# An attention and graph-convolution kernel: the output's scaling in two parts, one split earlier, and another order for the last two batches

## The chip, the cores and the metric

The kernel runs on one core of one Trainium2 chip. The metric is device time in microseconds; 0.2% of it (5.6 us) is about what a measurement of this kernel can tell from no change. Five engines work side by side, each through its own queue in order: TensorE (PE, with weight loads as PEld) multiplies matrices into the eight banks of PSUM, VectorE (DVE), ScalarE (ACT) and GpSimd (POOL) work element by element, and SyncE (SP) issues the transfers (DMA). [...]

## The reference

32 batches `x` of 512 rows by 512 features in float32 and one adjacency matrix `adj` (512 x 512, zeros and ones) that all share. Two layers follow each other, each with a residual and a normalisation of rows:

```python
# layer 0: masked attention of 8 heads of 64
q, k, v = x @ Wq + bq, x @ Wk + bk, x @ Wv + bv
scores = q k^T / 8 + where(adj == 0, -1e9, 0)
x = layernorm(x + softmax(scores) v)
# layer 1: graph convolution
x = layernorm(x + (adj @ x) @ weight + bias)
```

## The kernel before, in words

**Tiling.** A batch is four blocks of 128 rows (`NB`), its features four blocks of 128 (`DB`). Each of the three projections and the convolution with the weight is one Strassen-Winograd product of 2 x 2 blocks of 256: seven products (`block_product`, L369) of eight matmuls of 128x256 each, put together by additions on VectorE and GpSimd. A product's bank is emptied by VectorE (L391 to L404 in `project`, L537 and L541 in `convolve`) or ScalarE (L394, L535). `combine_rows` (L331 to L333, GpSimd) makes three of the seven left factors from the blocks of `xT` or `yT`.

**Attention.** The 8 heads are four pairs (`hp`), and two pairs are a group (`g`), so a batch has two groups. `scores` makes k q for a pair and block of keys (L568), VectorE adds the mask (L570), ScalarE exponentiates (L572), and GpSimd adds the four key blocks (L583); the second pair's additions are kept in `later`. `attend` multiplies with v (L592). `fold_squares` (L623, L625) and `add_up` (L633, L636) turn those sums into reciprocal row sums, `inverse`. `turn_out` brings a pair's output back to rows: VectorE transposes squares of 32 (L606) and sixteen small DMAs (L611) put them in place, in the tile `rows`. The second groups of batches 30 and 31 go another way: ScalarE copies the output (L603), and TensorE transposes it (L655).

**Residual.** `residual(b, hp)` scales `rows` by `inverse`, eight ScalarE instructions of 128x64 for a pair (L650), and adds them to `X[b]` on GpSimd (L651). In the other way VectorE does both from PSUM (L656, L657).

**Convolution.** Normalised rows are split into a high part in the rounded format float32r and a low rest: `split_high` on ScalarE (L457), `split_low` on VectorE (L461), which also adds the bias on GpSimd (L462). `aggregate` multiplies both parts with the adjacency (L488), four times for a batch; ScalarE copies the result to `yT` (L491), VectorE makes one more factor (L493). `convolve` is the product with the weight. Its first product also goes into the tile `mix` (ScalarE, L535), besides VectorE's addition to `X[b]` (L541); products 6 and 7 are added to `mix` (L537). Its order is 1, 2, 5, 6, 7, 3, 4.

**Order of the work.** The program fixes each engine's order by hand (`manual_schedule`): an engine runs its instructions in the order in which the program lists them. The loop goes over the 64 groups. It lists the group's attention, then the scores of the next group, then `units` of other batches' work:

- first group of batch b: projections q, k and the first two of v for batch b + 1, with statistics and normalisations of batches b - 1 and b - 2 in between;
- second group: the rest of v for batch b + 1, the four splits and aggregations of batch b - 1, its convolution, and the transposes (`turn_squares`, L353) of batch b + 2.

`units_of(b)` makes the list, `weighed` gives the units weights in steps of about half, and `work_until` takes them off until a share of the group's weight is done: 0.85 in the first group, 0.6 in the second. Then the two pairs' residuals come, then the rest. The second group's residuals therefore stand behind the fourth aggregation and in front of the convolution; the first group's behind the thirteenth projection. The fourth split stands behind the last of v.

The last batch has no projections. It takes batch 29's convolution and batch 30's aggregations in its first group's list, all of them before the last attention; batch 30's statistics come with its last residual, its normalisation and three of its `split_high` at the end of its list, and two `split_low` in the first attention of batch 31. After the loop come the last residuals, batch 30's convolution, and batch 31's normalisation, aggregation by rows (`aggregate_rows`, L515) and convolution.

Of the kernel before, what the change touches and what calls it, by code (L numbers as in the profile page):

```python
# [41 lines left out]
AF = mybir.ActivationFunctionType  # L42
# [5 lines left out]
P = 128  # L48
HD = 64
# [11 lines left out]
GROUP = 4  # L61
# [146 lines left out]
def fast_kernel(ctx: ExitStack, tc, verdict, x, adj, Wq, bq, Wk, bk, Wv, bv, W1, b1, out):  # L208
    nc = tc.nc
    B, N, D = x.shape  # L210
    H = Wq.shape[1] // HD
    HP = H // 2
    NB = N // P
    DB = D // P
# [8 lines left out]
    def bank(*shape):  # L223

        return psum.tile([P, *shape], FP, name="bank", tag="bank", bufs=8)


    X, IN = {}, {}
# [177 lines left out]
    def flips(b):  # L406

        return [(turn_squares if b else x_transpose, b, c) for c in range(NB)] + [(sum_rows, b)] if b < B else []
# [16 lines left out]
    def statistics(b, which, c):  # L425
        if b + which not in STAT:
            STAT[b + which] = work.tile([P, 2 * NB, 2], FP, name="stat", bufs=3)
            RSTD[b + which] = work.tile([P, 2 * NB], FP, name="rstd", bufs=3)
            SHIFT[b + which] = work.tile([P, 2 * NB], FP, name="shift", bufs=3)
        st = work.tile([P, nc.vector.BN_STATS_DIM], FP, name="bnst")  # L430
        nc.vector.bn_stats(st, X[b][:, c, :])  # L431
        nc.vector.bn_aggr(STAT[b + which][:, which * NB + c, :], st)  # L432
# [118 lines left out]
    def convolution(b):  # L551
        return [(convolve, b, i) for i in (1, 2, 5, 6, 7, 3, 4)] if b >= 0 else []
# [3 lines left out]
    PAIRS = GROUP // 2  # L556
# [41 lines left out]
    def turn_out(b, hp):  # L598

        po = OUT.pop((b, hp))  # L600
        at = AT[b, hp] = work.tile([P, N], FP, name="attT")
        if b >= B - 2 and hp >= PAIRS:
            nc.scalar.activation(at, po, AF.Copy)  # L603
            return

        nc.vector.transpose(at, po)  # L606
        turned = at.rearrange("p (c j f) -> p c j f", c=NB, j=P // SQ)
        rows = ROWS[b, hp] = work.tile([P, NB, P], FP, name="rows")
        for i in range(P // SQ):
            for j in range(P // SQ):  # L610
                nc.sync.dma_start(rows[j * SQ:(j + 1) * SQ, :, i * SQ:(i + 1) * SQ],  # L611
                                  turned[i * SQ:(i + 1) * SQ, :, j, :])
# [24 lines left out]
        nc.vector.tensor_add(sums, pm, sums)  # L637
        nc.gpsimd.tensor_add(inverses, inverses, inverse)

    def residual(b, hp):  # L640
        at = AT.pop((b, hp))
        first = 2 * hp % GROUP
        inverse = INVERSE[b, 2 * hp // GROUP][:, :, first:first + 2]
        cols = X[b][:, :, hp * P:(hp + 1) * P]
        if (b, hp) in ROWS:
            rows = ROWS.pop((b, hp))
            for c in range(NB):
                for s in range(2):
                    part = rows[:, c, s * HD:(s + 1) * HD]
                    nc.scalar.activation(part, part, AF.Identity, bias=zero, scale=inverse[:, c, s:s + 1])  # L650
            nc.gpsimd.tensor_add(cols, cols, rows)  # L651
        else:
            pt = bank(NB, 2, HD)
            for c in range(NB):
                nc.tensor.transpose(pt[:, c, :, :], at[:, c * P:(c + 1) * P], ident)  # L655
            nc.vector.tensor_mul(pt, pt, inverse[:, :, :, None].to_broadcast([P, NB, 2, HD]))  # L656
            nc.vector.tensor_add(cols, pt.rearrange("p c s d -> p c (s d)"), cols)  # L657
        if hp == HP - 1 and b == B - 2:
            for c in range(NB):
                statistics(b, 0, c)  # L660


    def judge():
# [12 lines left out]
    def run(units):  # L676
        for unit in units:
            unit[0](*unit[1:])
# [15 lines left out]
    def norm(t, which):  # L694

        if t - which < 0:
            return []
        lo, hi = which * NB, (which + 1) * NB
        return [(square_root, t, slice(lo, hi)), (invert_root, t, slice(lo, hi))] + [
            (normalise, t, slot) for slot in range(lo, hi)]  # L700

    def folds(b, g):
        return [(fold_squares, b, hp) for hp in range(g * PAIRS, (g + 1) * PAIRS)]

    def survey(b):

        return [(statistics, b, 1, c) for c in range(NB)] if b >= 0 else []

    def weighed(units):

        weight = {project: 0.5, aggregate: 0.55, x_transpose: 0.13, convolve: 0.5}
        return [(u, weight.get(u[0], 0.0)) for u in units]

    def units_of(b):

        made, turned = projections(b + 1), flips(b + 2)
        splits, gathered = aggregation(b - 1)
        young, old, seen = norm(b - 1, 0) if b < B - 1 else [], norm(b - 1, 1), survey(b - 2)
        ready = [(turn_over, b)] if 1 < b < B - 1 else []
        if b == B - 1:  # L720


            older = convolution(b - 2)
            lows = [(split_low, b - 1, d) for d in range(DB - 1)]
            last = folds(b, 1)
            units = weighed(older[:3] + last[:1] + lows[2:] + splits[3:] + older[3:] + gathered + last[1:] + seen)
            return units, [sum(w for _, w in units)] * 2

        fresh = [(statistics, b - 1, 0, c) for c in range(NB)] if young else []
        if old:  # L730
            behind = [seen[:2], seen[2:], old[:2], old[2:4] + fresh[:2], old[4:] + ready + fresh[2:]] + [
                [u] for u in young]
        else:
            behind = [ready + fresh] + [[u] for u in young]
        if b == 0:
            behind = [[]] + [[(sum_weights, w1, n)] for n in range(4)]
        behind += [[] for _ in range(11 - len(behind))] + [splits[:1], [], splits[1:2]]
        behind += [[] for _ in range(16 - len(behind))]
        units = []
        for k, unit in enumerate(made[:16]):  # L740
            units += [unit] + behind[k]
        first = sum(w for _, w in weighed(units))
        values = made[16:]
        looked = [(look_for_low_half, c) for c in range(NB)] if b == 0 else []
        units += values[:3] + looked[:2] + gathered[:1] + splits[2:3] + gathered[1:2] + values[3:] + looked[2:] + splits[3:]
        if b == B - 2 > 0:
            units += [(load, B - 1)]
        units += gathered[2:3] + turned[:1] + gathered[3:]
        convolved = convolution(b - 1) if b < B - 2 else []
        for k in range(7):  # L750
            units += convolved[k:k + 1] + (turned[k + 1:k + 2] if k < 3 else turned[4:] if k == 6 else [])
        units = weighed(units)
        return units, [first, sum(w for _, w in units)]

    GROUPS = H // GROUP
    groups = [(b, g) for b in range(B) for g in range(GROUPS)]
    for i, (b, g) in enumerate(groups):
        if g == 0:
            units, ends = units_of(b)
            done = 0.0  # L760

        def release():
            run(later)
            later.clear()

        def work_until(part):

            nonlocal done
            begin = ends[g - 1] if g else 0.0
            while units and (units[0][1] == 0 or done < begin + (ends[g] - begin) * part - 0.3):  # L770
                unit, w = units.pop(0)
                if unit[0] == fold_squares and unit[2] % PAIRS:
                    release()
                run([unit])
                done += w
                if unit[0] == (project if b < B - 1 else convolve):
                    if b == B - 1 or unit[3] == 7:
                        release()

        for hp in range(g * PAIRS, (g + 1) * PAIRS):  # L780
            attend(b, hp)
            if i < len(groups) - 1:
                fold_squares(b, hp)
            turn_out(b, hp)
            if hp == 0:
                run(flips(1) if i == 0 else [(split_low, b - 1, d) for d in range(2)] if i == len(groups) - 2 else [])
        if i == len(groups) - 1:
            add_up(b, g)
            break
        later = scores(*groups[i + 1])  # L790
        add_up(b, g)
        if g == 0 and b + 2 < B:
            load_squares(b + 2)
        work_until(0.6 if g else 0.85)
        for hp in range(g * PAIRS, (g + 1) * PAIRS):
            residual(b, hp)
        work_until(1.0)
        if g == GROUPS - 1:
            run([u for u, _ in units])
            if b == B - 2:  # L800
                run(norm(b, 0) + [(split_high, b, d) for d in range(DB - 1)])
        release()
    t = B - 1
    rest, last = convolution(t - 1), convolution(t)
    for hp in range(HP - PAIRS, HP):
        residual(t, hp)
    run(rest[:1])
    old, seen = norm(t - 1, 1), survey(t - 1)
    run(old[:1] + rest[1:2] + old[1:])
# [75 lines left out]
```

## Time and profile before

Time before: 2789.32 us, median of three runs (2787.78 to 2789.43); the profiled run's span is 2785.0 us.

| engine | busy us | share of the span | instructions |
|---|---|---|---|
| TensorE, matmuls | 2752.0 | 99% | 12850 |
| TensorE, weight loads | 1917.2 | 69% | 12850 |
| VectorE | 2033.2 | 73% | 3349 |
| GpSimd | 1898.1 | 68% | 1221 |
| ScalarE | 1406.0 | 50% | 2447 |

The 16 DMA engines are busy 22.8% of the span with 139.10 MB, much of it in small packets. The granted TensorE clock is 0.996. "L541 DVE" is the VectorE instruction of line 541; "x31" says how many there are. In a line with "|", the first numbers after it are busy us and mean ns of one, and the next the engine's idle time in front of it, with what ended it behind "<-". In a timeline the first number is the start in us from the span's start, the second how long the merged group ran, and an idle time of the engine in front of it stands in brackets. A matmul's duration in the trace is its latency, longer than its distance from the next; so what a stretch of TensorE costs is read from start to start.

### The profile page before, as it was taken

The numbers are of one execution on the slowest core, as the hardware profiler recorded it, in microseconds if no ns is written. First come the engines' busy times: TensorE is split into PE (matmuls) and PEld (weight loads), VectorE is DVE, ScalarE is ACT, GpSimd is POOL, SyncE is SP. The second block draws the span as 40 slices with busy tenths as digits, with TensorE's granted clock in tenths as the row PEclk, the third lists the DMA queues.
The fourth block names the chain that finished last, engine by engine and source line by source line (L and its number), as shares of the span: only waits on it lengthen the run. The fifth ranks groups of instructions, "written<-read, shape, count | busy, mean of one in ns | idle before, by whom it ended". The sixth has DMA issues, their size and how long they took to land. (4 is left out here: it accounts for less than half of the span.)

```text
span 2785.0 us, 39215 instructions
## 1 busy us (share of the span) xinstructions
PE 2752.0 (99%) x12850; PEld 1917.2 (69%) x12850; DVE 2033.2 (73%) x3349; ACT 1406.0 (50%) x2447; POOL 1898.1 (68%) x1221
## 2 busy tenths in 40 slices
PE   9999999999999999999999999999999999999997
PEld 6666766767767667667676676676766766767755
DVE  6777676687776777767867667777677676687777
ACT  2455544654545555445545455454555544654554
POOL 4666776767766668676677676677666767667764
PEclk9999999999999999999999999999999999999999
DMA  5112212222122222122221222211222212222111
GB/s 146 29 31 58 46 27 56 59 60 55 23 50 57 61 56 41 32 56 61 58 57 18 54 59 60 56 27 46 57 61 57 43 30 56 60 59 56 31 37 48
DMA packets 588305, 141.66 MB, mean 51 GB/s; under 512 B 549952, under 2 KB 554048, under 8 KB 588096
## 3 DMA queue, kind: packets, MB, share of 16 engines
q1 hardware_dynamic: 588096, 139.10, 22.8%
q8 instruction: 103, 1.69, 0.3%
q14 instruction: 106, 0.87, 0.1%
HBM read 72.88 MB, written 33.55 MB: 38 GB/s over the span
## 5 line engine op out<-in xcount | busy, mean ns | idle before, releaser
L572 ACT ACTIVATE e<-e 128x1024 f32<-128x1024 f32 x512 | 524.0, 1052 | 542.1 <-DVE e L570 516.4
L583 POOL TENSOR_TENSOR es<-es,e 128x1024 f32<-128x1024 f32 x256 | 617.7, 2413 | 20.1
L570 DVE SCALAR_TENSOR_TENSOR e<-gap,bank 128x512 f32<-128x512 uint8 x1024 | 616.7, 677 | 12.2 <-PE bank L568 12.2
L583 POOL TENSOR_TENSOR es<-e 128x1024 f32<-128x1024 f32 x128 | 316.1, 2469 | 302.3 <-ACT e L572 302.3
L568 PE MATMUL bank<-q,k 64*128 64x512 f32 x2048 | 477.3, 601 | 1.5 <-DVE attT L606 1.5
L592 PE MATMUL bank<-e,v 128*64 128x512 f32 x2048 | 456.0, 598 | 4.7 <-DVE v L404 4.7
L369 PE MATMUL bank<-wv,xT 128*128 128x256 f32 x1792 | 405.4, 381 | 0.0
L369 PE MATMUL bank<-xT,wk 128*128 128x256 f32 x1792 | 403.0, 379 | 0.7 <-DVE wk L319 0.7
L369 PE MATMUL bank<-xT,wq 128*128 128x256 f32 x1792 | 401.0, 381 | 2.5 <-DVE wq L319 1.7
L568 PEld LDWEIGHTS bank<-q,k 64*128 64x128 f32 x2048 | 212.9, 187 | 264.3 <-issue 141.4
L369 PE MATMUL bank<-w,yT 128*128 128x256 f32 x1792 | 392.3, 379 | 0.5 <-DVE yT L520 0.5
L369 PEld LDWEIGHTS bank<-w,yT 128*128 128x128 f32 x1792 | 340.0, 190 | 48.1 <-DVE yT L520 0.9
L369 PEld LDWEIGHTS bank<-xT,wk 128*128 128x128 f32 x1792 | 340.2, 190 | 47.2 <-PE bank L369 1.1
L369 PEld LDWEIGHTS bank<-xT,wq 128*128 128x128 f32 x1792 | 337.7, 190 | 49.1 <-POOL xT L333 1.8
L369 PEld LDWEIGHTS bank<-wv,xT 128*128 128x128 f32 x1792 | 337.5, 190 | 47.4 <-DVE e L570 0.8
L592 PEld LDWEIGHTS bank<-e,v 128*64 128x64 f32 x2048 | 142.0, 137 | 283.8 <-issue 277.4
L650 ACT ACTIVATE rows<-rows,zero,inverse 128x64 f32<-128x64 f32 x992 | 335.0, 428 | 3.5 <-DMA rows<-attT 3.4
L651 POOL TENSOR_TENSOR xs<-xs,rows 128x512 f32<-128x512 f32 x122 | 154.5, 1288 | 195.0 <-DMA xs<-in_x_dram 195.0
L572 ACT ACT_TABLE_LOAD x31 | 39.8, 1283 | 419.3 <-DVE e L570 419.3
L541 DVE TENSOR_TENSOR xs<-bank,xs 128x512 f32<-128x512 f32 x186 | 120.1, 672 | 157.1 <-ACT mix L535 156.9
L491 ACT ACTIVATE yT<-bank 128x512 f32<-128x512 f32 x124 | 74.0, 598 | 291.1 <-PE bank L488 291.1
L446 ACT ACTIVATE xs<-xs,shift,rstd 128x512 f32<-128x512 f32 x248 | 181.9, 803 | 27.3 <-DVE shift L441 25.8
(123 smaller groups left out, 3025.1 us busy)
## 6 DMA issues: line engine op xcount, KB each, us to landing
xin<-in_x_dram SPq DMA_DIRECT2D x496, 64.0 KB, 2.5
xs<-in_x_dram SPq DMA_DIRECT2D x31, 1024.0 KB, 5.2
rows<-attT SPq DMA_DIRECT2D x1984, 16.0 KB, 1.8
out_dram<-xs SPq DMA_DIRECT2D x31, 1024.0 KB, 4.4
xin<-in_x_dram SPq DMA_DIRECT2D x4, 256.0 KB, 3.4
wq<-in_L_gnn_Wq_dram SPq DMA_DIRECT2D x2, 512.0 KB, 5.8
wk<-in_L_gnn_Wk_dram SPq DMA_DIRECT2D x2, 512.0 KB, 8.2
yT<-in_adj_dram SPq DMA_DIRECT2D x1, 1024.0 KB, 8.1
```

The source lines that it names most:

```text
L369: nc.tensor.matmul(pm[:, r, :], left[:, d, r * P:(r + 1) * P], right[:, d, :], start=(d == 0), stop=(d == 1))
L446: nc.scalar.activation(row, row, AF.Identity, bias=SHIFT[t][:, slot:slot + 1], scale=RSTD[t][:, slot:slot + 1])
L491: nc.scalar.activation(yt[:, d // 2:d // 2 + 3:2, d % 2, :], pm, AF.Copy)
L541: nc.vector.tensor_add(block, pm, block)
L568: nc.tensor.matmul(ps[s], keys[:, j * P:(j + 1) * P], queries, start=True, stop=True)
L570: nc.vector.scalar_tensor_tensor(e[:, s, :], gap[:, j, :], NEG * root, ps[s], op0=ALU.mult, op1=ALU.add)
L572: nc.scalar.activation(e, e, AF.Exp, scale=1.0 / root)
L583: nc.gpsimd.tensor_add(ES[b, hp], ES[b, hp] if j > 1 else E[b, hp, 0], E[b, hp, j])
L592: nc.tensor.matmul(po[s * HD:(s + 1) * HD, :], values, e[:, s, :], start=(j == 0), stop=(j == NB - 1))
L650: nc.scalar.activation(part, part, AF.Identity, bias=zero, scale=inverse[:, c, s:s + 1])
L651: nc.gpsimd.tensor_add(cols, cols, rows)
```

## The change

It does four things.

1. `residual` becomes two units, `scale_rows` (ScalarE, L650) and `add_rows` (GpSimd, L651), that stand in the lists like other work. In the second group the third pair's scaling is listed behind the fourth split, before the last of v; the fourth pair's behind the convolution's first product. The third pair's addition follows there, the fourth pair's stands behind the convolution. This is for ScalarE, so that the first product's copy to `mix` isn't behind sixteen scalings. In the first group both stay behind the thirteenth projection.
2. The fourth split is listed right behind the second aggregation, in front of the last of v.
3. The last two batches are ordered anew. Batch 30's second group takes the usual way through DMA; only batch 31's second group is transposed by TensorE (`last_residual`). Batch 30's statistics, normalisation and splits are put behind the products of batch 29's convolution, and batch 30's aggregations come after the last attention, with batch 31's scaling and batch 29's statistics behind them.
4. The weights and `work_until` go; `merge` puts two lists together unit by unit, and each group has a list of its own (`slots`).

The diff, cut to its core:

```diff
@@ turn_out
-        if b >= B - 2 and hp >= PAIRS:
+        if (b, hp // PAIRS) == (B - 1, HP // PAIRS - 1):
             nc.scalar.activation(at, po, AF.Copy)
             return
@@ residual
+    def scale_rows(b, hp):
+        rows, inverse = ROWS[b, hp], inverse_of(b, hp)
+        for c in range(NB):
+            for s in range(2):
+                part = rows[:, c, s * HD:(s + 1) * HD]
+                nc.scalar.activation(part, part, AF.Identity, bias=zero, scale=inverse[:, c, s:s + 1])
+
+    def add_rows(b, hp):
         cols = X[b][:, :, hp * P:(hp + 1) * P]
+        nc.gpsimd.tensor_add(cols, cols, ROWS.pop((b, hp)))
...
-        if hp == HP - 1 and b == B - 2:
-            for c in range(NB):
-                statistics(b, 0, c)
@@ units_of
+    def residuals(b, g):
+
+        return [[(f, b, hp) for hp in range(g * PAIRS, (g + 1) * PAIRS)] for f in (scale_rows, add_rows)]
...
         if b == B - 1:
-            older = convolution(b - 2)
-            lows = [(split_low, b - 1, d) for d in range(DB - 1)]
-            last = folds(b, 1)
-            units = weighed(older[:3] + last[:1] + lows[2:] + splits[3:] + older[3:] + gathered + last[1:] + seen)
-            return units, [sum(w for _, w in units)] * 2
+            first, second = folds(b, 1)
+            behind = [fresh[:2], fresh[2:], young[:1], young[1:3], young[3:5] + [first], young[5:] + splits[:1],
+                      splits[1:]]
+            return [merge(convolution(b - 2), behind), [second] + merge(gathered, [scaled, added, seen[:2], seen[2:]])]
...
-        behind += [[] for _ in range(11 - len(behind))] + [splits[:1], [], splits[1:2]]
+        behind += [[] for _ in range(11 - len(behind))]
+        behind += [splits[:1], scaled + added, splits[1:2]]
...
-        units += values[:3] + looked[:2] + gathered[:1] + splits[2:3] + gathered[1:2] + values[3:] + looked[2:] + splits[3:]
+        scaled, added = residuals(b, 1)
+        slot1 = values[:3] + looked[:2] + gathered[:1] + splits[2:3] + gathered[1:2] + splits[3:] + scaled[:1]
+        slot1 += values[3:] + looked[2:]
         if b == B - 2 > 0:
-            units += [(load, B - 1)]
-        units += gathered[2:3] + turned[:1] + gathered[3:]
+            slot1 += [(load, B - 1)]
+        slot1 += gathered[2:3] + turned[:1] + gathered[3:]
         convolved = convolution(b - 1) if b < B - 2 else []
-        for k in range(7):
-            units += convolved[k:k + 1] + (turned[k + 1:k + 2] if k < 3 else turned[4:] if k == 6 else [])
+        slot1 += merge(convolved, [scaled[1:] + added[:1] + turned[1:2], turned[2:3], turned[3:4], [], [], [],
+                                   added[1:] + turned[4:]])
@@ the loop
-        work_until(0.6 if g else 0.85)
-        for hp in range(g * PAIRS, (g + 1) * PAIRS):
-            residual(b, hp)
-        work_until(1.0)
-        if g == GROUPS - 1:
-            run([u for u, _ in units])
-            if b == B - 2:
-                run(norm(b, 0) + [(split_high, b, d) for d in range(DB - 1)])
-        release()
+        for unit in slots[g]:
+            run([unit])
+            if unit[0] == convolve or unit[0] == project and unit[3] == 7:
+                run(later)
+                later = []
+        run(later)
+        later = []
```

More of the change, by code (lines that the diff above doesn't have):

```diff
@@ L638, in add_up, with inverse_of, last_residual @@
         nc.gpsimd.tensor_add(inverses, inverses, inverse)
-    def residual(b, hp):
-        at = AT.pop((b, hp))
+    def inverse_of(b, hp):
         first = 2 * hp % GROUP
-        inverse = INVERSE[b, 2 * hp // GROUP][:, :, first:first + 2]
-        cols = X[b][:, :, hp * P:(hp + 1) * P]
-        if (b, hp) in ROWS:
-            rows = ROWS.pop((b, hp))
-            for c in range(NB):
[L648 to L657, printed above, removed]
-        if hp == HP - 1 and b == B - 2:
-            for c in range(NB):
-                statistics(b, 0, c)
+        return INVERSE[b, 2 * hp // GROUP][:, :, first:first + 2]
+    def scale_rows(b, hp):
[5 more added lines that the diff above has]
+    def add_rows(b, hp):
+        cols = X[b][:, :, hp * P:(hp + 1) * P]
+        nc.gpsimd.tensor_add(cols, cols, ROWS.pop((b, hp)))
+    def last_residual(b, hp):
+        pt = bank(NB, 2, HD)
+        for c in range(NB):
+            nc.tensor.transpose(pt[:, c, :, :], AT[b, hp][:, c * P:(c + 1) * P], ident)
+        nc.vector.tensor_mul(pt, pt, inverse_of(b, hp)[:, :, :, None].to_broadcast([P, NB, 2, HD]))
+        cols = X[b][:, :, hp * P:(hp + 1) * P]
+        nc.vector.tensor_add(cols, pt.rearrange("p c s d -> p c (s d)"), cols)
     def judge():
@@ L707, in survey, with merge @@
         return [(statistics, b, 1, c) for c in range(NB)] if b >= 0 else []
-    def weighed(units):
-        weight = {project: 0.5, aggregate: 0.55, x_transpose: 0.13, convolve: 0.5}
-        return [(u, weight.get(u[0], 0.0)) for u in units]
+    def residuals(b, g):
+        return [[(f, b, hp) for hp in range(g * PAIRS, (g + 1) * PAIRS)] for f in (scale_rows, add_rows)]
+    def merge(units, behind):
+        merged = []
+        for k in range(max(len(units), len(behind))):
+            merged += units[k:k + 1] + (behind[k] if k < len(behind) else [])
+        return merged
     def units_of(b):
@@ L717, in units_of @@
         splits, gathered = aggregation(b - 1)
-        young, old, seen = norm(b - 1, 0) if b < B - 1 else [], norm(b - 1, 1), survey(b - 2)
-        ready = [(turn_over, b)] if 1 < b < B - 1 else []
+        old, seen = norm(b - 1, 1), survey(b - 2)
+        fresh, young = ([(statistics, b - 1, 0, c) for c in range(NB)], norm(b - 1, 0)) if b else ([], [])
+        scaled, added = residuals(b, 0)
         if b == B - 1:
-            older = convolution(b - 2)
-            lows = [(split_low, b - 1, d) for d in range(DB - 1)]
-            last = folds(b, 1)
-            units = weighed(older[:3] + last[:1] + lows[2:] + splits[3:] + older[3:] + gathered + last[1:] + seen)
-            return units, [sum(w for _, w in units)] * 2
-        fresh = [(statistics, b - 1, 0, c) for c in range(NB)] if young else []
+            first, second = folds(b, 1)
+            behind = [fresh[:2], fresh[2:], young[:1], young[1:3], young[3:5] + [first], young[5:] + splits[:1],
+                      splits[1:]]
+            return [merge(convolution(b - 2), behind), [second] + merge(gathered, [scaled, added, seen[:2], seen[2:]])]
+        ready = [(turn_over, b)] if b > 1 else []
         if old:
@@ L732, in units_of @@
                 [u] for u in young]
-        else:
-            behind = [ready + fresh] + [[u] for u in young]
-        if b == 0:
+        elif b:
+            behind = [ready + fresh] + [[u] for u in young]
+        else:
             behind = [[]] + [[(sum_weights, w1, n)] for n in range(4)]
-        behind += [[] for _ in range(11 - len(behind))] + [splits[:1], [], splits[1:2]]
[L738 to L742, printed above, removed]
+        behind += [[] for _ in range(11 - len(behind))]
+        behind += [splits[:1], scaled + added, splits[1:2]]
+        slot0 = merge(made[:16], behind)
         values = made[16:]
         looked = [(look_for_low_half, c) for c in range(NB)] if b == 0 else []
-        units += values[:3] + looked[:2] + gathered[:1] + splits[2:3] + gathered[1:2] + values[3:] + looked[2:] + splits[3:]
+        scaled, added = residuals(b, 1)
+        slot1 = values[:3] + looked[:2] + gathered[:1] + splits[2:3] + gathered[1:2] + splits[3:] + scaled[:1]
+        slot1 += values[3:] + looked[2:]
         if b == B - 2 > 0:
-            units += [(load, B - 1)]
-        units += gathered[2:3] + turned[:1] + gathered[3:]
+            slot1 += [(load, B - 1)]
+        slot1 += gathered[2:3] + turned[:1] + gathered[3:]
         convolved = convolution(b - 1) if b < B - 2 else []
-        for k in range(7):
-            units += convolved[k:k + 1] + (turned[k + 1:k + 2] if k < 3 else turned[4:] if k == 6 else [])
-        units = weighed(units)
-        return units, [first, sum(w for _, w in units)]
+        slot1 += merge(convolved, [scaled[1:] + added[:1] + turned[1:2], turned[2:3], turned[3:4], [], [], [],
+                                   added[1:] + turned[4:]])
+        return [slot0, slot1]
     GROUPS = H // GROUP
@@ L757, in fast_kernel @@
     for i, (b, g) in enumerate(groups):
[L758 to L772, printed above, removed]
-                    release()
[L774 to L778, printed above, removed]
         for hp in range(g * PAIRS, (g + 1) * PAIRS):
@@ L784, in fast_kernel @@
             turn_out(b, hp)
-            if hp == 0:
-                run(flips(1) if i == 0 else [(split_low, b - 1, d) for d in range(2)] if i == len(groups) - 2 else [])
-        if i == len(groups) - 1:
+            if i == hp == 0:
+                run(flips(1))
+        if g == 0:
+            slots = units_of(b)
+        if i < len(groups) - 1:
+            later = scores(*groups[i + 1])
             add_up(b, g)
-            break
-        later = scores(*groups[i + 1])
-        add_up(b, g)
         if g == 0 and b + 2 < B:
             load_squares(b + 2)
-        work_until(0.6 if g else 0.85)
-        for hp in range(g * PAIRS, (g + 1) * PAIRS):
-            residual(b, hp)
-        work_until(1.0)
-        if g == GROUPS - 1:
-            run([u for u, _ in units])
-            if b == B - 2:
-                run(norm(b, 0) + [(split_high, b, d) for d in range(DB - 1)])
-        release()
+        for unit in slots[g]:
[5 more added lines that the diff above has]
+        later = []
+    add_up(B - 1, GROUPS - 1)
     t = B - 1
@@ L805, in fast_kernel @@
     for hp in range(HP - PAIRS, HP):
-        residual(t, hp)
+        last_residual(t, hp)
     run(rest[:1])
```

## The prediction

> **What bounds the kernel now.** I read the page first, then the timeline of TensorE, then those of the engines that TensorE waits for, then the end of the run.
>
> ```profile
> PE 2752.0 (99%) x12850; PEld 1917.2 (69%) x12850; DVE 2033.2 (73%) x3349; ACT 1406.0 (50%) x2447; POOL 1898.1 (68%) x1221
> ...
> L541 DVE TENSOR_TENSOR xs<-bank,xs 128x512 f32<-128x512 f32 x186 | 120.1, 672 | 157.1 <-ACT mix L535 156.9
> ```
>
> TensorE decides: 99% busy, and the other engines matter only where they hold it up. But 99% doesn't mean that only 1% is to be had: an instruction that starts late inside a run of matmuls leaves no idle time that this row shows. So I measured from start to start. One steady batch, timeline of TensorE (start, us, group):
>
> ```profile
> 1038.63 7.21 PE L568 MATMUL bank<-q,k 64*128 64x512 f32 x32
> 1045.77 0.26 PE L633 MATMUL bank<-part,fold 128*32 128x16 f32 x8
> ...
> 1051.05 1.28 PE L488 MATMUL bank<-adjT,low 128*128 128x512 f32 x4
> ...
> 1054.97 3.61 PE L369 MATMUL bank<-wv,xT 128*128 128x256 f32 x16
> 1058.23 1.29 PE L488 MATMUL bank<-adjT,low 128*128 128x512 f32 x4
> 1059.36 1.10 PE L488 MATMUL bank<-adjT,high 128*128 128x512 f32 x4
> 1060.52 1.17 PE L488 MATMUL bank<-adjT,low 128*128 128x512 f32 x4
> ...
> 1062.45 12.25 PE L369 MATMUL bank<-w,yT 128*128 128x256 f32 x56
> 1074.63 7.09 PE L592 MATMUL bank<-e,v 128*64 128x512 f32 x32
> 1081.65 7.51 PE L568 MATMUL bank<-q,k 64*128 64x512 f32 x32
> 1089.09 0.26 PE L633 MATMUL bank<-part,fold 128*32 128x16 f32 x8
> ```
>
> Two places lose time in every batch. Aggregations 0 and 1 (sixteen matmuls of L488) take 1054.97 - 1051.05 = 3.92 us, aggregations 2 and 3 take 1062.45 - 1058.23 = 4.22: 0.31 more, at 1060.52, where the fourth `low` is read. The scores (L568) of the second group take 1045.77 - 1038.63 = 7.14, those of the next batch's first group 1089.09 - 1081.65 = 7.44: 0.30 more. Over the whole trace the first loss stands 29 times (sum 9.15 us), the second 29 times (sum 9.0). Who makes them, from the timelines of ScalarE and VectorE in that batch:
>
> ```profile
> 1063.15 5.40 ACT L650 ACTIVATE rows<-rows,zero,inverse 128x64 f32<-128x64 f32 x16
> 1068.44 0.58 ACT L535 ACTIVATE mix<-bank 128x512 f32<-128x512 f32 x1
> ```
>
> ```profile
> 1059.29 1.09 DVE L461 TENSOR_TENSOR low<-xs,high 128x512 fp32r<-128x512 f32 x1
> ...
> 1069.06 0.69 DVE L541 TENSOR_TENSOR xs<-bank,xs 128x512 f32<-128x512 f32 x1 [5.35 <-ACT mix L535]
> ```
>
> The sixteen scalings stand in front of the copy of the first product (L535); VectorE's first addition (L541) waits 5.35 us for that copy, so VectorE enters the next attention behind its work and starts the masks (L570) at 1083.15, 1.5 us after the scores began; in the second group it is 1.16 (1039.79 - 1038.63). The fourth `low` ends at 1059.29 + 1.09 = 1060.38, and the matmul that reads it starts at 1060.52: VectorE does it only after two evictions of v.
>
> The end of the run, timeline of TensorE:
>
> ```profile
> 2684.64 1.09 PE L488 MATMUL bank<-adjT,high 128*128 128x512 f32 x4
> 2688.59 1.18 PE L488 MATMUL bank<-adjT,low 128*128 128x512 f32 x4 [2.86 <-DVE low L461]
> ...
> 2691.40 7.89 PE L592 MATMUL bank<-e,v 128*64 128x512 f32 x32
> 2699.22 3.70 PE L568 MATMUL bank<-q,k 64*128 64x512 f32 x14
> 2703.25 5.88 PE L568 MATMUL bank<-q,k 64*128 64x512 f32 x18 [0.33 <-DVE attT L606]
> 2709.06 0.26 PE L633 MATMUL bank<-part,fold 128*32 128x16 f32 x8
> ```
>
> Against the steady durations (3.91, 7.02, 7.14) aggregations 2 and 3 here lose 3.97 (0.87 of it the transposes of L655 between them), the attention 0.80, the scores 2.70.
>
> [...]
>
> **The change part by part.** Steady batches first, in the clock of the batch above.
>
> *Fourth split forward.* ScalarE's fourth `high` ends at 1056.28 already (1055.66 + 0.62). VectorE then does the fourth `low` at 1056.3 to 1057.0 (0.69 when undisturbed, up to 1.17 beside GpSimd), before it evicts v. TensorE wants it at 1060.3. Loss of 0.31 gone; v's eviction at 1056.96 slips by under 0.5 us and its bank is not asked for so soon. 29 x 0.315 = -9.15 us.
>
> *Scaling in two parts.* Eight scalings take 5.40/2 = 2.7 us. The first eight run from 1056.3 to 1059.0, in ScalarE's idle 4.21 us before the eviction of aggregation 2 at 1060.49. They need the rows of the third pair: 32 DMA issues take 20.60 us from 1036.09, so half are out by 1046.4 and landed 1.8 us later, at 1048.2: 8 us early. The new wait of ScalarE on that DMA holds nothing up. Then the first product's copy runs as soon as TensorE has it: 1062.45 + 8 x 0.216 + about 0.4 of latency = 1064.5, done at 1065.1 instead of 1069.02. VectorE's additions follow TensorE from there, and its last one is done at 1075.6 (TensorE's last product, 1074.63, plus 0.3, plus 0.65), so the folds begin about 1.1 us after the attention, as in the second group (1032.74 after 1031.61): scores 7.14. The other eight scalings, 1065.1 to 1067.8, stand before nothing. GpSimd's addition of the fourth pair comes 1.3 us before the sums of the next xT, which then end near 1083.3, about where they end now (1083.6), 6 us before the projections ask. Loss of 0.30 gone: -9.0 us.
>
> *First group's scaling.* Same place (after 13 of 16 projections) and same order on each engine: 0.
>
> *The end.* Batch 30's second group goes the usual way through DMA, so 8 transposes (0.87) and four VectorE operations leave. Its normalising and the splits move behind batch 29's convolution, and the last attention comes before the aggregations. TensorE without waits, from 2679.38: v 3.26, aggregations 3.91, attention 7.02, scores 7.14, row sums 0.19, convolution 12.2, attention 7.0, four aggregations 7.8, row sums and transposes 1.1: it reaches the next convolution at 2729.0, today 2737.28: -8.3. Are the splits in time? VectorE ends the sixteen masks (0.603 each, from 1.2 after the attention's end, 2693.6) at 2704.5 and the row sums at 2704.9. The first product's copy waits for the last exponential (1.05) and is done at 2706.2. Then VectorE has seven additions 4.4, statistics 3.2, roots 0.35, a fold 2.45, a wait of about 1.5 for GpSimd (six additions of row weights at 2.41 end near 2713, then L539) and the first `low` 1.0: 2719.1. The other three, 0.9 to 2.0 each, follow at 2720.6, 2722.6, 2724.6; wanted at 2720.1, 2722.1, 2724.0, 2726.0. In time, by 1.0 to 1.5. But the last batch's 16 scalings (5.4) now stand behind aggregation 0's eviction (2723.0) and before the next three: 2728.4, two evictions 2729.4, then on VectorE two additions of 0.4 and four statistics of 0.8 in turn, row sums 0.35: L656 starts at 2733.8. Today it is at 2738.54 and from there the chain of waits runs on VectorE to `low` L503 (2749.23), which the last aggregation waits for. So 4.7 of the 8.3 us arrive. The rest becomes a longer wait of L515 than today's 0.74.
>
> *Startup.* VectorE's wait of 4.54 us at the low-half test is for attention's output buffer, which its DMA still reads; its place in VectorE's queue is the same: 0.
>
> Sum: 9.15 + 9.0 + 4.7 = 22.9 us; 2789.32 - 22.9 = 2766.4.
>
> **The rivals.**
> - *One of the two steady losses stays*, because what ends last there is another thing (a bank, GpSimd at 16.1 of 16.5 us busy in the stretch 1045.96 to 1062.45). For it: GpSimd has no room there. Against: neither matmul reads what GpSimd writes there. 2789.32 - 9.1 - 4.7 = 2775.5.
> - *The end gains all or nothing*: the last `low`s have only 1 to 1.5 us of room. 2789.32 - 18.2 - 8.3 = 2762.8, or 2789.32 - 18.2 = 2771.1.
> - *TensorE doesn't get faster*, since both waits only change their name. Against: the second group's scores show 7.14, with the same code and VectorE on time. About 2786.
> - *Slower*: the scalings put forward block ScalarE on late rows, so aggregation 2's eviction and the products behind it slip. 1 us in each of 29 batches would give 2789.32 - 22.9 + 29 = 2795. Against: 8 us of room.
>
> **How the numbers follow.** Forecast with the end near 4.7: 0.66. The end at all or nothing: 0.16. One loss stays: 0.10. No change that can be told: 0.03. Slower: 0.05. The range reaches from somewhat under full gain, 2761, to just short of "one loss stays", 2775; it leaves out 0.18. Faster 0.92, same 0.03, slower 0.05.
>
> **What would show it.** Right: all scores in steady batches at 7.14 and all pairs of aggregations at 3.92; VectorE's wait for L535 down from 156.9 to some 45 us (1.5 each); eight L650 on each side of L535; a batch 0.61 us shorter (85.50 to 84.89); at the end, no wait at the fourth `low`, and L515 waiting 3 to 4 us. Wrong: a new wait of ScalarE for the rows' DMA, or scores still at 7.44 with the folds early.

## The result, and the profile after

The changed kernel takes 2765.05 us (median of four runs, 2764.76 to 2765.34) against 2789.12 us in the same comparison: a ratio of 0.9915, 95% interval 0.9897 to 0.9932. That is 24.1 us less, where 22.9 were forecast; the spans of the two profiled runs, 2785.0 and 2762.9 us, are 22.1 apart. In the numbers of the page:

```profile
PE 2735.6 (99%) x12842; PEld 1912.7 (69%) x12842; DVE 2068.2 (75%) x3347; ACT 1411.1 (51%) x2459; POOL 1902.6 (69%) x1223
...
L568 PE MATMUL bank<-q,k 64*128 64x512 f32 x2048 | 465.2, 599 | 0.0
```

TensorE was 99% busy and is 99% busy; the row doesn't show that 22 us went. The group of the scores does: the same 2048 matmuls of L568 were busy 477.3 us before and are 465.2 now. And the waits of VectorE and ScalarE around the first product, from the view of all waits (engine, who waited for whom, us in total, times, longest):

```profile
DVE xs L541 <- ACT mix L535: 39.2, 30, 1.5
ACT mix L535 <- PE bank L369: 36.3, 31, 2.3
```

VectorE's wait for the copy fell from 156.9 to 39.2 us, and ScalarE now waits for TensorE in front of that copy, as it should. One steady batch after, timelines of TensorE, ScalarE and VectorE (start, us, group):

```profile
1048.69 3.61 PE L369 MATMUL bank<-wv,xT 128*128 128x256 f32 x16
1051.95 1.29 PE L488 MATMUL bank<-adjT,low 128*128 128x512 f32 x4
1053.08 1.09 PE L488 MATMUL bank<-adjT,high 128*128 128x512 f32 x4
1054.01 1.09 PE L488 MATMUL bank<-adjT,low 128*128 128x512 f32 x4
1054.94 1.09 PE L488 MATMUL bank<-adjT,high 128*128 128x512 f32 x4
1055.88 12.25 PE L369 MATMUL bank<-w,yT 128*128 128x256 f32 x56
1068.05 7.09 PE L592 MATMUL bank<-e,v 128*64 128x512 f32 x32
1075.07 7.21 PE L568 MATMUL bank<-q,k 64*128 64x512 f32 x32
1082.21 0.26 PE L633 MATMUL bank<-part,fold 128*32 128x16 f32 x8
```

```profile
1049.38 0.62 ACT L457 ACTIVATE high<-xs 128x512 fp32r<-128x512 f32 x1
1049.90 2.75 ACT L649 ACTIVATE rows<-rows,zero,inverse 128x64 f32<-128x64 f32 x8
1054.21 0.60 ACT L491 ACTIVATE yT<-bank 128x512 f32<-128x512 f32 x1 [1.57 <-PE bank L488]
1056.07 0.60 ACT L491 ACTIVATE yT<-bank 128x512 f32<-128x512 f32 x1 [1.26 <-PE bank L488]
1057.80 0.60 ACT L535 ACTIVATE mix<-bank 128x512 f32<-128x512 f32 x1 [1.13 <-PE bank L369]
1058.29 2.75 ACT L649 ACTIVATE rows<-rows,zero,inverse 128x64 f32<-128x64 f32 x8
```

```profile
1050.03 1.60 DVE L461 TENSOR_TENSOR low<-xs,high 128x512 fp32r<-128x512 f32 x1 [1.17 <-ACT high L457]
...
1058.43 0.69 DVE L541 TENSOR_TENSOR xs<-bank,xs 128x512 f32<-128x512 f32 x1 [1.30 <-ACT mix L535]
...
1069.18 1.25 DVE L623 STREAM_TRANSPOSE e<-es 128x1024 f32<-128x1024 f32 x1 [0.33 <-PE bank L592]
```

(The scalings are now L649.) Aggregations 2 and 3 take 1055.88 - 1051.95 = 3.93 us (4.22 before), the scores 1082.21 - 1075.07 = 7.14 (7.44 before). The fourth `low` is done at 1051.63, 2.4 us before TensorE's start at 1054.01. VectorE begins the fold 1.13 us after the attention and waits for TensorE there, no longer the other way round. From start to start of this attention a batch takes 84.89 us in the mean of the next 18, against 85.50.

The end, TensorE again, last the stretch that had 0.74 us of wait:

```profile
2667.91 1.09 PE L488 MATMUL bank<-adjT,high 128*128 128x512 f32 x4
2668.93 7.09 PE L592 MATMUL bank<-e,v 128*64 128x512 f32 x32
2675.94 7.21 PE L568 MATMUL bank<-q,k 64*128 64x512 f32 x32
...
2711.37 12.25 PE L369 MATMUL bank<-w,yT 128*128 128x256 f32 x56
2727.58 0.76 PE L515 MATMUL bank<-adjT,low 128*128 128x512 f32 x1 [3.96 <-DVE low L503]
2728.15 0.63 PE L515 MATMUL bank<-adjT,high 128*128 128x512 f32 x1
2728.57 0.63 PE L515 MATMUL bank<-adjT,low 128*128 128x512 f32 x1
```

The waits at the fourth `low`, the attention and the scores are gone (7.02 and 7.14 us), and instead TensorE waits 3.96 us at L515.

### The profile page after: what moved, and what is told of

Read it like the earlier page. It is cut to its first block, busy times and chain, and to the rows that moved or that the text cites. A ratio compares the mean times of both kernels' runs of the same rounds, so it can differ in the third digit from the quotient of the medians.

```text
span 2762.9 us, 39328 instructions
## 1 busy us (share of the span) xinstructions
PE 2735.6 (99%) x12842; PEld 1912.7 (69%) x12842; DVE 2068.2 (75%) x3347; ACT 1411.1 (51%) x2459; POOL 1902.6 (69%) x1223
## 4 chain that ended last, share of the span: by engine, by line
PE 97%; DVE 1%; SPq 1%; ACT 0%; DMA 0%; issue 0%; POOL 0%; DVEq 0%; ACTq 0%
PE bank L369 55%; PE bank L568 16%; PE bank L592 16%; PE bank L488 8%; SPq L611 1%; PE bank L633 0%; DVE bnst L431 0%; DMA wq<-in_L_gnn_Wq_dram 0%; ACT rows L649 0%; PE bank L515 0%; DVE xT L541 0%; DVE part L816 0%; DVE xs L541 0%; DVE xT L506 0%; DVE low L503 0%
## 5 line engine op out<-in xcount | busy, mean ns | idle before, releaser
L583 POOL TENSOR_TENSOR es<-es,e 128x1024 f32<-128x1024 f32 x256 | 618.2, 2415 | 20.1
L583 POOL TENSOR_TENSOR es<-e 128x1024 f32<-128x1024 f32 x128 | 315.9, 2468 | 333.0 <-ACT e L572 333.0
L568 PE MATMUL bank<-q,k 64*128 64x512 f32 x2048 | 465.2, 599 | 0.0
L568 PEld LDWEIGHTS bank<-q,k 64*128 64x128 f32 x2048 | 204.0, 186 | 259.6 <-issue 160.4
L649 ACT ACTIVATE rows<-rows,zero,inverse 128x64 f32<-128x64 f32 x1008 | 343.2, 427 | 0.0
L461 DVE TENSOR_TENSOR low<-xs,high 128x512 fp32r<-128x512 f32 x122 | 143.5, 1176 | 104.2 <-ACT high L457 104.2
```

The costliest lines, as they stand in the source:

```text
L461: nc.vector.tensor_sub(LOW[b, d], cols, HIGH[b, d].bitcast(FP))
L568: nc.tensor.matmul(ps[s], keys[:, j * P:(j + 1) * P], queries, start=True, stop=True)
L583: nc.gpsimd.tensor_add(ES[b, hp], ES[b, hp] if j > 1 else E[b, hp, 0], E[b, hp, j])
```

## The experiments

The diffs are against the changed kernel, those of the last two experiments against the run before them, and they touch `units_of` alone, where nothing else is said. Each ratio is to the kernel before in the same comparison: 2788.72 us beside the first four kernels, which share a chip, and 2787.51 beside the last four, on another. The changed kernel itself was in neither of these comparisons, so "above" and "under the changed kernel" are differences from its 2765.05 us. In each of the two one kernel takes the same time as it (2764.55 and 2764.58 us), and against that one the differences are within 0.6 us of those given.

**The fourth split back behind the last of v.**

```diff
-        slot1 = ... + gathered[1:2] + splits[3:] + scaled[:1]
-        slot1 += values[3:] + looked[2:]
+        slot1 = ... + gathered[1:2]
+        slot1 += scaled[:1] + values[3:] + looked[2:] if b == 0 else values[3:] + splits[3:] + scaled[:1]
```

> The changed kernel with only the fourth split back behind the last of v (batches 1 to 30); every queue but VectorE's keeps its order. Theory (two losses that are independent of each other): the second pair of aggregations loses 0.31 us in 29 batches again, the scores stay at 7.14: 2765.0 + 9.2 = 2774.2, ratio to the kernel before 0.9946. Rival (the early scalings alone free enough of VectorE that the order no longer matters): 2765.

Measured: 2775.31 us, ratio 0.9956 (0.9943 to 0.997), that is 10.3 us above the changed kernel. The pair of aggregations loses 0.32 to 0.34 us in each steady batch again (once 0.63), 9.9 us in all; the scores stay at 7.14. TensorE, ScalarE and GpSimd run their instructions in the same order as in the changed kernel from the first to the last. VectorE, timeline:

```profile
1055.65 0.69 DVE L404 TENSOR_TENSOR v<-bank,v 128x512 f32<-128x512 f32 x1 [1.02 <-PE bank L369]
1056.26 1.10 DVE L461 TENSOR_TENSOR low<-xs,high 128x512 fp32r<-128x512 f32 x1
```

`low` stands behind v's eviction again and ends at 1057.36; TensorE's matmuls that read it start at 1057.51. Only the order in VectorE's queue differs, so the 0.3 us a batch belong to it.

**Both pairs scaled in front of the convolution again.**

```diff
-        slot1 = ... + splits[3:] + scaled[:1]
+        slot1 = ... + splits[3:] + (scaled[:1] if b == 0 else [])
...
-        slot1 += merge(convolved, [scaled[1:] + added[:1] + turned[1:2], turned[2:3], ..., added[1:] + turned[4:]])
+        slot1 += (scaled[1:] if b == 0 else scaled) + added + merge(convolved, [turned[1:2], turned[2:3], ..., turned[4:]])
```

> The changed kernel with both pairs of the second group scaled and added again in front of the convolution (batches 1 to 30), the fourth split left forward. Theory: VectorE waits some 5 us for the copy of the first product again, the scores of the first groups lose 0.30 us in 29 batches, aggregations stay at 3.92: 2765.0 + 9.0 = 2774.0, ratio 0.9946. Rival (TensorE has slack for VectorE's delay once the split is forward): 2765.

Measured: 2774.62 us, ratio 0.9949 (0.9936 to 0.9963), 9.6 us above. The scores of the first groups lose 0.31 to 0.32 us again (twice 0.48), the aggregations nothing. The wait comes back whole, as the view of all waits has it:

```profile
DVE xs L541 <- ACT mix L535: 157.4, 30, 5.5
```

GpSimd's additions move with the scalings in this run, and no run moves them apart. VectorE's wait for GpSimd next to them (L537 for L539) is 41.4 us in all here and 41.3 in the changed kernel, so they aren't what holds VectorE up.

**Both taken back** (the two edits together).

> Both taken back in the steady batches; what stays of the change is the order of the last two batches. Theory: 2765.0 + 18.2 = 2783.2, that is 4 to 5 us under the kernel before, ratio 0.9980. Rival (the losses overlap, so that taking back both costs little more than one): 2774. Rival (the end gives nothing, the steady part all): 2789.

Measured: 2784.26 us, ratio 0.9984 (0.9978 to 0.9991), 19.2 us above the changed kernel; the two single losses, 10.3 and 9.6, sum to 19.9. The two gains add up, to within 0.7 us. What stays, 2788.72 - 2784.26 = 4.5 us, belongs to the new order of the last two batches (4.7 forecast); the interval of the ratio puts it at 2.5 to 6.1 us, and the stretch from the v projections of batch 30's second group to the end is 3.9 us shorter than before in the trace.

**All sixteen scalings behind the first product's copy.**

```diff
-        ... + splits[3:] + scaled[:1]
+        ... + splits[3:] + (scaled[:1] if b == 0 else [])
...
-        slot1 += merge(convolved, [scaled[1:] + added[:1] + ...
+        slot1 += merge(convolved, [(scaled[1:] if b == 0 else scaled) + added[:1] + ...
```

> All sixteen scalings of the second group behind the first product's copy, none in front of the fourth aggregation: not in two parts. Theory (all that matters is that none stands between the fourth eviction and that copy): the copy runs at once, the scalings end about 5.5 us behind it, GpSimd adds the third pair's rows after its three sums of yT, as now: 2765, ratio 0.9915. Rival (the parting itself is needed, because sixteen scalings there delay GpSimd's additions and with them products 6 and 7): a loss of some 0.3 us a batch or more, 2774 or above.

Measured: 2764.55 us, ratio 0.9915 (0.9902 to 0.9929): no difference. Sixteen scalings run from 1058.29 to 1063.70 there, GpSimd adds the third pair's rows at 1062.50, 0.03 us from where it does in the changed kernel: that engine was busy until then. The two parts are not what brings the gain.

**All sixteen right behind the fourth split.**

```diff
-        ... + splits[3:] + scaled[:1]
+        ... + splits[3:] + (scaled[:1] if b == 0 else scaled)
...
-        slot1 += merge(convolved, [scaled[1:] + added[:1] + ...
+        slot1 += merge(convolved, [(scaled[1:] if b == 0 else []) + added[:1] + ...
```

> All sixteen scalings of the second group right behind the fourth split, in front of the eviction of the third aggregation. Theory: the fourth pair's rows have landed by then (issue of 32 transfers 20.6 us from the third pair's transpose, landing 1.8 us later, about when the first eight scalings end), so the third eviction comes 1.2 us later, which the second convolution product, 1.7 us behind the first, doesn't feel: 2765, ratio 0.9915. Rival (ScalarE stands in front of rows not yet landed and passes that on through the evictions to the products): 1 us in each of 29 batches, 2794.

Measured: 2764.58 us, ratio 0.9918 (0.9905 to 0.9932): no difference either. ScalarE's timeline:

```profile
1049.19 5.41 ACT L649 ACTIVATE rows<-rows,zero,inverse 128x64 f32<-128x64 f32 x16
1054.50 0.58 ACT L491 ACTIVATE yT<-bank 128x512 f32<-128x512 f32 x1
1055.35 0.60 ACT L491 ACTIVATE yT<-bank 128x512 f32<-128x512 f32 x1 [0.27 <-PE bank L488]
1057.08 0.60 ACT L535 ACTIVATE mix<-bank 128x512 f32<-128x512 f32 x1 [1.13 <-PE bank L369]
```

All sixteen run without a pause, so the rows had landed, and only the third eviction slips. The margin is nearly used up: three times ScalarE did wait for the rows' DMA, 2.5 us together, as the view of L649 shows. The rival that forecast a slower kernel is out all the same; in the changed kernel L649 waits for no DMA anywhere.

**The last batch's scaling moved out of the way.**

```diff
-            behind = [fresh[:2], ..., splits[1:]]
-            return [merge(convolution(b - 2), behind), [second] + merge(gathered, [scaled, added, seen[:2], seen[2:]])]
+            behind = [fresh[:2] + scaled[:1], ..., splits[1:] + scaled[1:]]
+            return [merge(convolution(b - 2), behind), [second] + merge(gathered, [[], added, seen[:2], seen[2:]])]
```

> The changed kernel with the last batch's first-group scalings moved out of the way: the first pair's behind the first product of batch 29's convolution, the second pair's behind batch 30's last split. Theory (these sixteen scalings, 5.4 us between the evictions of aggregations 0 and 1 of batch 30, are what kept 3.6 of the 8.3 us at the end): the last three evictions follow TensorE, VectorE starts the last residual 2 us earlier relative to the aggregations, and the wait at L515 falls from 3.96 to about 1.9: 2765.0 - 2.0 = 2763.0, ratio 0.9906. If the slow matmuls after that wait (0.43 us apart instead of 0.23, 1.4 us in all) go with it: 2761.6. Rival (the chain on VectorE is bound by its own work there): 2765.

Measured: 2760.60 us, ratio 0.9903 (0.9888 to 0.9918), 4.5 us under the changed kernel. The evictions follow TensorE, and TensorE waits 1.42 us at L515:

```profile
2711.09 12.25 PE L369 MATMUL bank<-w,yT 128*128 128x256 f32 x56
2724.77 0.47 PE L515 MATMUL bank<-adjT,low 128*128 128x512 f32 x1 [1.42 <-DVE low L503]
2725.07 0.40 PE L515 MATMUL bank<-adjT,high 128*128 128x512 f32 x1
2725.31 0.40 PE L515 MATMUL bank<-adjT,low 128*128 128x512 f32 x1
```

The wait is 2.5 us shorter, and the L515 matmuls are 0.23 us apart at once, where the changed kernel has them 0.43 apart for the first seven: the 32 take 8.08 us instead of 9.44. Together 3.9 of the 4.5 us; against the kernel with all sixteen scalings early, in the same comparison, the difference is 4.0 (four runs from 2760.53 to 2760.83 us against five from 2763.86 to 2765.42). So the scalings were what kept back most of the rest of the end's gain, and the estimate of 2.0 us plus 1.4 was a little short.

**Batch 29's last statistics earlier as well.**

```diff
-            ... [second] + merge(gathered, [[], added, seen[:2], seen[2:]])]
+            ... [second] + merge(gathered, [[], seen + added, [], []])]
```

> As the run before, and batch 29's last statistics (3.2 us of VectorE) in front of the eviction of the third aggregation, where VectorE waits 2.98 us in the changed kernel. Theory: VectorE starts the last residual another 0.8 us earlier, and the wait at L515 is about 1.1 us; with it the slow matmuls go: 2765.0 - 2.8 - 1.4 = 2760.8, ratio 0.9899. Rival (only the order counts, VectorE's work stays the same): as the run before.

Measured: 2760.23 us, ratio 0.9902 (0.9886 to 0.9917): 0.4 us under the run before it, which these runs can't tell from nothing. The trace has the wait at L515 at 0.92 instead of 1.42 us, so the direction is right. The 2.2 us forecast were not there: 1.4 of them, the slow matmuls, had already gone with the run before, and of the 0.8 us for the wait the trace shows 0.5.

**The test of the adjacency's low half in batch 0's first group.**

```diff
@@ look_for_low_half
-        cut = work.tile([P, N], FP, name="attT")
+        cut = work.tile([P, N], FP, name="low")
@@ units_of, batch 0
             behind = [[]] + [[(sum_weights, w1, n)] for n in range(4)]
+            for c in range(NB):
+                behind += [[(look_for_low_half, c)]]
+                if c % 2:
+                    behind += [[]]
...
-        slot1 = values[:3] + looked[:2] + gathered[:1] + ... + values[3:] + looked[2:]
+        slot1 = values[:3] + gathered[:1] + ... + values[3:]
```

> As the run before, and the test of the adjacency's low half in the first group of batch 0, with a buffer of its own instead of attention's output buffer. Theory (VectorE's wait for the DMA that still reads that buffer, and the test's own 6.7 us of VectorE, make TensorE lose 7.6 us in the attention and 2.3 in the scores of the third group): most of the 9.8 us go: 2760.8 - 9.0 = 2751.8, ratio 0.9866. Rival (the first groups lose the same time to other VectorE work that then comes late): 2760.

Measured: 2751.69 us, ratio 0.9871 (0.9856 to 0.9886), 13.4 us under the changed kernel and 8.5 under the run before. TensorE's timeline in the stretch where both kernels waited 4.7 us for v:

```profile
115.65 8.90 PE L369 MATMUL bank<-wv,xT 128*128 128x256 f32 x40
124.48 7.09 PE L592 MATMUL bank<-e,v 128*64 128x512 f32 x32
131.50 8.22 PE L568 MATMUL bank<-q,k 64*128 64x512 f32 x32
139.64 0.26 PE L633 MATMUL bank<-part,fold 128*32 128x16 f32 x8
```

The attention takes 7.02 us, where it took 14.58 in the changed kernel; the scores 8.14 instead of 9.40. The run changes the buffer and the place of the test together, so it doesn't tell which of them counts. A part of the gain is TensorE's clock: in the changed kernel it was granted at half for 6.8 us in this stretch (0.50 from 129.6 to 136.4 us), and the last 24 matmuls of the attention took 7.96 us, where three quarters of the 7.02 are 5.27. The mean granted clock of the whole profiled run is 0.999 here and 0.997 in the run before it. This part has nothing to do with the change.

## Why the prediction was right

*Fourth split, 9.15 us.* In the trace 29 losses of 0.31 us became 29 of at most 0.02; taking it back alone costs 10.3. The step was right. One size in it was off: `low` took 1.60 us, while GpSimd was adding (L583), not 0.69 to 1.17 (0.68 where GpSimd did nothing, in 15 of the changed kernel's 122), and v's eviction began at 1051.55 instead of near the end of its product, 0.9 us later, measured from its product. The eviction after it was on time again.

*Scaling, 9.0 us.* Right in place and size: 9.6 when taken back alone, scores at 7.14, VectorE's wait at 39.2 us (some 45 forecast). But "in two parts" was not needed. The runs with all sixteen behind the copy and with all sixteen ahead of the evictions take the same time. In all three kernels that keep the gain none of them stands between the fourth eviction and the copy; before, all 5.4 us stood there. How many could stand there without harm, no run shows. VectorE waits for the copy with and without them: 1.5 us at most in these three kernels, 5.5 in the kernel before and in the run with both pairs in front of the convolution. Why it waits for the copy at all, no run tests.

*First group, startup: 0.* The sum is right: the projections behind the startup's last scores begin at 148.57 us, 148.49 before. Inside that stretch times did move: the last attention and scores ahead of them took 24.67 us before and 23.98 after, from a start 0.77 us later. That is within what one program does from run to run: the run with both pairs scaled early again and the one with both edits taken back are the same program up to there and took 24.68 and 23.98.

*The end, 4.7 us.* Measured 4.5 by the run with both steady parts taken back, and 4.4 in the trace: from the v projections of batch 30's second group to the end of the span, 2785.0 - 2670.37 = 114.63 before, 2762.9 - 2652.65 = 110.25 after. The path was the one forecast. VectorE begins the last residual 63.2 us behind those projections, 68.2 before: 5.0 earlier, 4.7 forecast. These are its first instructions, before and after:

```profile
2738.54 0.70 DVE L656 TENSOR_TENSOR bank<-bank,inverse 128x512 f32<-128x512 f32 x1
```

```profile
2715.86 0.70 DVE L660 TENSOR_TENSOR bank<-bank,inverse 128x512 f32<-128x512 f32 x1
```

TensorE waits 3.96 us at L515, "3 to 4" forecast. What the sum left out is that TensorE came out of that wait slow, which costs 1.36 us. Against it stands, by luck, that the closing of the program behind VectorE's last computation was 0.8 us shorter in the changed kernel's profiled run (2762.9 - 2755.90 = 7.0, 2785.0 - 2777.23 = 7.8). Together they take 0.6 us off the 5.0.

One reading of the end was wrong. The prediction put 0.87 us of what aggregations 2 and 3 lost there down to transposes of L655 between them. Those transposes stand in front of v, at 2679.38 us, and none lies between the aggregations. Besides the wait of 2.86 us there is a slow clock, granted at half from 2689.6 to 2693.1 us (lines in the last section). With it the last four matmuls of L488 take 1.79 us to the attention, where the changed kernel has 1.02 (2667.91 to 2668.93), and the attention loses its 0.80. The sum of 8.3 us is right all the same: it was counted from 2679.38, and the transposes take 0.87 us there.

*The sum.* The trace splits into 17.8 us in the steady batches (2670.37 - 148.49 = 2521.88, 2652.65 - 148.57 = 2504.08), 4.4 at the end and -0.1 at the start: 22.1. The forecast said 18.2, 4.7 and 0. The medians are 24.1 apart, 2 us more than the spans: the profiled run of the kernel before took 2786.9 us, 2.2 under its median, that of the changed kernel 2764.78, 0.3 under. The interval of the ratio, 19 to 29 us, holds both.

*The rivals.* One loss staying would have been 2775.5: the two single runs show what that looks like. The end gained neither all nor nothing, 4.4 to 4.5 of 8.3 us. A new wait of ScalarE for the rows' DMA isn't in the changed kernel's trace, and the run that asked for the rows earliest had it three times and lost nothing measurable.

## What to carry to other kernels

An engine that a page calls 99% busy can still lose time in every round (0.6 us of 85.5 here): measure the same block of work in two places of a round, start to start, and the difference is what a late neighbour costs. Long work without a near deadline, such as these scalings, belongs in its engine's queue where the engine waits anyway, and never in front of a short copy that another engine waits for (5.35 us of VectorE here, for a copy of 0.58); splitting it is one way, moving it whole is as good. At the end of a run, where work no longer overlaps, look at what stands in front of each short link of the last chain, and check the granted clock behind a long wait of TensorE: the one of 3.96 us cost 1.36 us more than its length.

## What the runs showed of the hardware

At some of its waits TensorE's granted clock fell to 0.50, for 3.4 or 6.8 us. In the changed kernel, views of stretches behind the 3.96 us wait (us, busy time and count of each engine, granted clock, DMA share, GB/s):

```profile
2727.50:2730.50 3.00, 2.92 (x7) 2.37 (x8) 1.74 (x3) 1.09 (x2) 1.66 (x1) 0.50 0.02 5
2730.50:2737.00 6.50, 6.17 (x26) 4.71 (x26) 4.66 (x7) 2.81 (x5) 1.30 (x1) 1.00 0.00 0
```

The granted clock is 0.50 for one piece of 3.4 us (2727.1 to 2730.5; the wait ended at 2727.58) and 1.00 after it; the matmuls are 0.43 us apart, then 0.23, with 0.63 and 0.40 us as their durations. The kernel before has the same behind its wait of 2.86 us at the fourth `low`, which ended at 2688.59:

```profile
2689.70:2693.00 3.30, 3.30 (x9) 1.39 (x9) 0.43 (x1) 1.47 (x2) 0.46 (x2) 0.50 0.02 5
2693.10:2699.00 5.90, 5.90 (x30) 1.82 (x26) 4.50 (x6) 4.33 (x8) 3.28 (x3) 1.00 0.00 0
```

It has it in the startup too, at the wait of 4.67 us that ended at 130.24 (the granted clock is 0.50 from 129.7 to 133.0 us), and again from 143.3 to 146.7 us (0.50), 1.5 us behind the end of a wait of only 1.19. After the waits at L515 of 0.74 us (kernel before), 1.42 and 0.92 us (the two runs with the last batch's scaling moved) nothing of the kind shows: behind all three the matmuls are 0.23 to 0.24 us apart from the second on, and the granted clock is 1.00 behind the first two (2750.3 to 2756.3 and 2724.8 to 2728.0 us). So the clock fell behind waits of 2.86 and of 1.19 us, and not behind one of 1.42: the length of a wait alone doesn't tell whether the clock falls, and what else decides is not tested here. The prediction, which foresaw the wait of 3 to 4 us and had these slow pieces in the trace of the kernel before, should have allowed for one more.
